# Cross-attention and a quantized feed-forward block: the order of loads, stores and row sums in a hand-written loop

## The chip, the cores and the metric

The kernel runs on one core of a Trainium2 chip. The time is device microseconds of one execution. A profiled execution gives a page and a trace beside it.

## The reference

The input x has 4 batches of 2048 rows of 512 values. Two layers follow one another.

```python
x = x + xattn(layernorm(x), ctx_1024, Wq, Wkv, Wout, bout)
x = x + ffn(layernorm(x), w1, b1, w2, b2, gamma, beta)
```

In the attention the mask lets a query i see only the keys j with `j % n_q == i`. There are 2048 queries and 154 keys, so query i < 154 sees one key, its own, and every other query sees none of them and averages all. The layer's result for a row of x is therefore a row that depends on the context alone: the row of value i for i < 154, the mean row for the rest. The kernel computes these rows once and adds them to x.

The feed-forward layer normalizes a row (with gamma and beta), quantizes it to whole numbers by its largest absolute value, multiplies by w1 (512 to 2048, weights quantized to -1, 0 and 1), rescales and adds b1, applies GELU, quantizes the 2048 values of the row in the same way, multiplies by w2 (2048 to 512), rescales, adds b2, and adds the result to x.

## The kernel before

The 8192 rows are 64 tiles of 128 rows, taken in the order `seq`. All constants stay in SBUF. Every engine runs its instructions in the order of a text: the strings BEGINNING, STEADY and ENDING hold words, and each word calls one function for one tile. BEGINNING prepares the weights and the context rows and runs up to tile 23. A loop over n = 24, 28, ... 52 runs STEADY, in which a number is counted from n: U2 is the word U for tile n+2. ENDING takes the last eight tiles. Nothing reorders the words afterwards. Words on different engines run side by side as their data allows; words on the same engine stand in line.

For one tile the words are, in the order of its life:

- L: load two tiles of x, 512 KB (`load_pair`, SyncE's DMA queue, L199). In STEADY, L14 loads tiles n+14 and n+15, and L16 loads n+16 and n+17.
- a: add the context row to x (`add_rows`, GpSimd, L269). S: mean and variance (VectorE, L276, L277). N: reciprocal roots for four tiles (GpSimd).
- k, e: normalize, gamma and beta (GpSimd, L323, L326, L327). R: largest value (VectorE, L355; for the last of four tiles also L361, L363). v: scales of four tiles (VectorE, L369, L371). X: add b2 to x (GpSimd, L349).
- Q: quantize the row (ScalarE, L375). T: transpose it by DMA to `xqT` (SyncE's queue, L386).
- I: put b1 into PSUM, in two halves (I n.half.vector; VectorE L545 or ScalarE L547). U: 16 matmuls with w1 (TensorE, L555).
- G: GELU, in two halves (ScalarE, L574). M: largest value of a half (VectorE, L586, then L600 to L603). D: a scale (GpSimd, L608).
- H: quantize 2048 values (ScalarE, L615). h: transpose them by DMA to `hqT`, 512 KB (SyncE's queue, L626).
- W: 16 matmuls with w2 (TensorE, L633). F: rescale and add to x (VectorE, L639). f: store the tile, 256 KB (SyncE's queue, L642).

Beside these, s and t load context rows for a later batch; they follow STEADY at n = 28 and 44 (s) and at n = 24 (t).

All DMAs of the loop are issued by SyncE, in the order of the words L, T, h, f, s and t, and each issue waits for its data. So a word that is not ready holds up those behind it. U of a tile needs its T; W needs its h.

Of the kernel before, what the change touches and what calls it, by code (L numbers as in the profile page):

```python
# [53 lines left out]
def xattn_ffn(ctx: ExitStack, tc, x, ctxT, WvT, Wout, bout, w1T, b1, w2T, b2, gamma, beta, out):  # L54
    nc = tc.nc
    B, S, D = x.shape
# [20 lines left out]
    for g, size in enumerate(sizes):  # L77
# [64 lines left out]
    """  # L142
    STEADY = """
        U0 W-2 G0.0 I1.0.1 G0.1 M0.0 Q2 k7 I1.1.0 T2 M0.1
        U1 L14 e7 L16 G1.0 X0 H0 M1.0 W-1 a13 I2.0.1 Q3 h0 D-1 S11 G1.1 a15 T3 R6 I2.1.0
        U2 N8 M1.1 G2.0 F-2 D0 R7 D1 a14 H1 W0 v4 I3.0.1 k9 G2.1 h1 X3 M2.0 I3.1.0 a12 F-1
        U3 Q4 M2.1 e9 I4.0.0 T4 S12 H2 F0 k8 W1 S13 X1 G3.0 h2 G3.1 M3.0 e8 I4.1.0 M3.1 Q5
        k10 T5 S14 H3 e10 f-2 f-1 F1 f0 R8 h3 R9 f1 X2 D2
    """
    ENDING = """  # L150
        U0 k7 W-2 I1.0.1 G0.0 e7 G0.1 M0.0 I1.1.0 M0.1 D-1 X1 Q2
# [622 lines left out]
```

## Time and profile before

| | |
|---|---|
| median of three runs | 523.04 us (521.98 to 523.38) |
| the profiled execution | 520.9 us, span 519.1 us |
| TensorE busy | 500.0 us |
| VectorE, ScalarE, GpSimd busy | 425.0, 420.4, 395.8 us |
| transposes of GELU rows (L626) | 65, median 4.4 us from issue to landing |
| loads of x (L199) | 32, median 5.4 us |
| stores (L642) | 64, median 2.5 us |
| granted TensorE clock | 0.997 |

Lines of a group give line, engine, operation, what it writes and reads, the count, then busy time and mean duration. In the chain of waits each piece has its start, its length and what it was; a timeline has start, length, engine, line and operation. A matmul of 512 columns follows the one before after 0.216 us in the trace although the page gives it 379 ns, since matmuls overlap; a busy TensorE is therefore not yet one without gaps.

### The profile page before, as it was taken

Reading aid. Unit: us, or ns where it says so; the run is one execution under the profiler, and the core shown is the slowest. Engines: PE = TensorE matmul, PEld = TensorE weight load, DVE = VectorE, ACT = ScalarE, POOL = GpSimd, SP = SyncE. Lnnn points to the kernel's source line nnn. Section 1 sums busy time; section 2 is a strip of 40 time slices with the busy share of each in tenths; the row PEclk is TensorE's granted clock in tenths of the full one; section 3 lists DMA queues with packets and bytes.
Section 4 is the critical chain, followed back from the end, with each engine's and each line's share of the span. In section 5 each row is a group of like instructions: output and inputs, shape, how many; then the busy total and the mean of one; then the engine's idle time right before and its main releaser. Section 6 shows DMA issues by size and latency. Waiting matters only on the chain.

```text
span 519.1 us, 6893 instructions
## 1 busy us (share of the span) xinstructions
PE 500.0 (96%) x2168; PEld 222.2 (43%) x2168; DVE 425.0 (82%) x757; ACT 420.4 (81%) x386; POOL 395.8 (76%) x512
## 2 busy tenths in 40 slices
PE   9796999999999999999989999999999999999996
PEld 4342444444444434444434444444444444444442
DVE  0478999999989797798988798989889978796762
ACT  1275999999898989878889697788787887998971
POOL 0048999999999979789969899996999599942120
PEclk9998999999999999999999999999999999999999
DMA  8998457797558899586696968679766876685654
GB/s 284 398 390 310 152 106 179 170 235 149 157 110 176 219 226 235 100 202 153 131 234 121 254 96 231 101 181 185 182 156 125 196 155 130 92 212 133 142 110 125
DMA packets 194114, 94.00 MB, mean 181 GB/s; under 512 B 170269, under 2 KB 170269, under 8 KB 194077
## 3 DMA queue, kind: packets, MB, share of 16 engines
q1 hardware_dynamic: 194076, 93.56, 74.7%
q8 instruction: 17, 0.28, 0.2%
q14 instruction: 21, 0.16, 0.1%
HBM read 34.55 MB, written 17.04 MB: 99 GB/s over the span
## 4 chain that ended last, share of the span: by engine, by line
PE 68%; DMA 18%; DVE 8%; ACT 2%; POOL 1%; issue 1%; SPq 0%; ACTq 0%; POOLq 0%; DVEq 0%
PE po L633 32%; PE ph L555 32%; DMA hqT<-hq 12%; DMA wo<-Wout_dram 3%; DVE m L586 2%; PE py L465 2%; DMA ws<-w2T_dram 2%; DVE ph L545 1%; ACT hid L574 1%; DVE m L355 1%; DMA wv<-WvT_dram 1%; POOL x L269 1%; DVE x L639 1%; DVE bn L276 1%; PE py_mean L465 1%
## 5 line engine op out<-in xcount | busy, mean ns | idle before, releaser
L633 PE MATMUL po<-w2q,hqT 128*128 128x512 f16 x1024 | 231.3, 379 | 5.2 <-DMA hqT<-hq 5.2
L555 PE MATMUL ph<-w1q,xqT 128*128 128x512 f16 x1024 | 231.5, 379 | 1.0 <-DMA xqT<-xqg 0.6
L586 DVE TENSOR_REDUCE m<-hid 128x1 f32<-128x1024 f32 (+1 forms) x130 | 153.4, 1194 | 39.7 <-ACT hid L574 39.2
L574 ACT ACTIVATE hid<-ph,d 128x1024 f32<-128x1024 f32 (+1 forms) x130 | 140.2, 1092 | 38.4 <-PE ph L555 26.8
L633 PEld LDWEIGHTS <-hqT 128*128 128x128 f16 x1024 | 99.1, 98 | 129.1 <-DMA hqT<-hq 11.3
L555 PEld LDWEIGHTS <-xqT 128*128 128x128 f16 x1024 | 100.1, 98 | 124.5 <-issue 2.8
L615 ACT ACTIVATE hq<-hid,i 128x2048 f16<-128x2048 f32 (+1 forms) x65 | 128.0, 1970 | 18.5 <-DVE i L603 8.8
L547 ACT ACTIVATE ph<-b_b,inv 128x1024 f32<-128x1024 f32 x91 | 100.5, 1112 | 1.2 <-POOL inv L369 0.8
L349 POOL TENSOR_TENSOR x<-x,b_b 128x512 f32<-128x512 f32 x59 | 74.8, 1270 | 0.0
L269 POOL TENSOR_TENSOR x<-x,mean 128x512 f32<-128x512 f32 x51 | 65.1, 1280 | 11.2 <-DMA x<-x_dram 9.5
L327 POOL TENSOR_TENSOR h<-h,beta_b 128x512 f32<-128x512 f32 x50 | 63.8, 1275 | 3.9
L326 POOL TENSOR_TENSOR h<-h,gamma_b 128x512 f32<-128x512 f32 x50 | 63.5, 1270 | 1.8
L639 DVE SCALAR_TENSOR_TENSOR x<-po,d,x 128x512 f32<-128x512 f32 x64 | 47.1, 739 | 10.9 <-PE po L633 10.6
L375 ACT ACTIVATE xqg<-h,s 128x512 f16<-128x512 f32 x64 | 45.2, 713 | 3.2 <-DVE s L363 3.2
L545 DVE TENSOR_SCALAR ph<-b_b,inv 128x1024 f32<-128x1024 f32 x37 | 47.3, 1277 | 0.0
L276 DVE BATCH_NORM_STATS2 bn<-x 128x6 f32<-128x512 f32 x64 | 43.6, 681 | 3.3 <-POOL x L269 3.2
L355 DVE TENSOR_REDUCE m<-h 128x1 f32<-128x512 f32 x64 | 41.9, 672 | 1.7 <-POOL h L327 1.4
L608 POOL TENSOR_TENSOR d<-mh,wm 128x1 f32<-128x1 f32 x64 | 12.6, 205 | 39.0 <-DVE mh L601 35.1
L323 POOL TENSOR_SCALAR h<-x,minus,rstd 128x512 f32<-128x512 f32 x50 | 38.4, 768 | 0.4
L436 PE MATMUL wps<-wo,wv 128*128 128x512 f32 x64 | 28.5, 597 | 1.8 <-DMA wv<-WvT_dram 1.4
L245 POOL TENSOR_SCALAR w1q<-wi 128x1024 f16<-128x1024 int16 x5 | 5.7, 1149 | 31.7 <-ACT wi L242 31.7
L251 DVE TENSOR_REDUCE part<-ws 128x1 f32<-128x1024 f32 x7 | 8.1, 1209 | 19.5 <-DMA ws<-w1T_dram 19.5
(75 smaller groups left out, 273.4 us busy)
## 6 DMA issues: line engine op xcount, KB each, us to landing
x<-x_dram SPq DMA_DIRECT2D x32, 512.0 KB, 5.4
out_dram<-x SPq DMA_DIRECT2D x64, 256.0 KB, 2.5
ws<-w1T_dram SPq DMA_DIRECT2D x8, 512.0 KB
ws<-w2T_dram SPq DMA_DIRECT2D x8, 512.0 KB, 8.7
wv<-WvT_dram SPq DMA_DIRECT2D x8, 256.0 KB, 7.8
wo<-Wout_dram SPq DMA_DIRECT2D x8, 256.0 KB, 6.6
ctx_sb<-ctxT_dram SPq DMA_DIRECT2D x1, 1232.0 KB
hqT<-hq SPq DMA_TRANSPOSE x65, 4.4
```

What stands on the lines that cost most here:

```text
L269: e.tensor_tensor(x_of(n), x_of(n), y, ALU.add)
L326: nc.gpsimd.tensor_tensor(normed[n], normed[n], gamma_b, ALU.mult)
L327: nc.gpsimd.tensor_tensor(normed[n], normed[n], beta_b, ALU.add)
L349: e.tensor_tensor(x_of(n), x_of(n), b2_b, ALU.add)
L545: nc.vector.tensor_scalar(ph, row, d, None, ALU.mult)
L547: nc.scalar.activation(ph, row, AF.Identity, bias=0.0, scale=d)
L555: nc.tensor.matmul(bank[i], xqT[n][:, k, :], w1q[:, k, i * 512 : (i + 1) * 512], start=False, stop=(k == KD - 1), skip_group_check=True,)
L574: nc.scalar.activation(hidden[n][:, i * w : (i + 1) * w], up_ps[n][half][:, lo : lo + w], AF.Gelu, bias=0.0, scale=deq1[g][:, j : j + 1],)
L586: nc.vector.tensor_reduce(m2[:, i : i + 1], hidden[n][:, i * w : (i + 1) * w], AX.X, ALU.max, apply_absolute_value=True,)
L615: nc.scalar.activation(hq[n][:, lo : lo + w], hidden[n][:, lo : lo + w], AF.Identity, bias=0.0, scale=inv2[n],)
L633: nc.tensor.matmul(po, hqT[n][:, k, :], w2q[:, k, :], start=(k == 0), stop=(k == KH - 1))
L639: nc.vector.scalar_tensor_tensor(t, down_ps.pop(n), deq2[n], t, ALU.mult, ALU.add)
```

## The change

Only the text STEADY changes. Before it, the loads L14 and L16 stand together near the start of U1, ahead of h0; after it, L14 stands behind h0 and L16 behind h1. The four sums of x with the row, `a13 a15 a14 a12` before, become `a12 a13 a14 a15`, in the same four places. The stores f-2 and f-1 move from behind T5 to behind h2, ahead of T5; f0 moves from ahead of h3 to behind it.

```diff
     STEADY = """
         U0 W-2 G0.0 I1.0.1 G0.1 M0.0 Q2 k7 I1.1.0 T2 M0.1
-        U1 L14 e7 L16 G1.0 X0 H0 M1.0 W-1 a13 I2.0.1 Q3 h0 D-1 S11 G1.1 a15 T3 R6 I2.1.0
-        U2 N8 M1.1 G2.0 F-2 D0 R7 D1 a14 H1 W0 v4 I3.0.1 k9 G2.1 h1 X3 M2.0 I3.1.0 a12 F-1
-        U3 Q4 M2.1 e9 I4.0.0 T4 S12 H2 F0 k8 W1 S13 X1 G3.0 h2 G3.1 M3.0 e8 I4.1.0 M3.1 Q5
-        k10 T5 S14 H3 e10 f-2 f-1 F1 f0 R8 h3 R9 f1 X2 D2
+        U1 e7 G1.0 X0 H0 M1.0 W-1 a12 I2.0.1 Q3 h0 L14 D-1 S11 G1.1 a13 T3 R6 I2.1.0
+        U2 N8 M1.1 G2.0 F-2 D0 R7 D1 a14 H1 W0 v4 I3.0.1 k9 G2.1 h1 L16 X3 M2.0 I3.1.0 a15
+        F-1
+        U3 Q4 M2.1 e9 I4.0.0 T4 S12 H2 F0 k8 W1 S13 X1 G3.0 h2 f-2 f-1 G3.1 M3.0 e8 I4.1.0
+        M3.1 Q5 k10 T5 S14 H3 e10 F1 R8 h3 f0 f1 R9 X2 D2
     """
```

SyncE's queue in one iteration, before and after:

```
before: T2 L14 L16 h0 T3 h1 T4 h2 T5 f-2 f-1 f0 h3 f1
after:  T2 h0 L14 T3 h1 L16 T4 h2 f-2 f-1 T5 h3 f0 f1
```

GpSimd's, before and after; VectorE, ScalarE and TensorE keep theirs:

```
before: k7 e7 X0 a13 D-1 a15 N8 D0 D1 a14 k9 X3 a12 e9 k8 X1 e8 k10 e10 X2 D2
after:  k7 e7 X0 a12 D-1 a13 N8 D0 D1 a14 k9 X3 a15 e9 k8 X1 e8 k10 e10 X2 D2
```

## The prediction

> **What bounds the kernel now.** I read the page first: its busy shares, its chain of waits and its DMA issues.
>
> ```profile
> PE 500.0 (96%) x2168; PEld 222.2 (43%) x2168; DVE 425.0 (82%) x757; ACT 420.4 (81%) x386; POOL 395.8 (76%) x512
> PE 68%; DMA 18%; DVE 8%; ACT 2%; POOL 1%; issue 1%; SPq 0%; ACTq 0%; POOLq 0%; DVEq 0%
> hqT<-hq SPq DMA_TRANSPOSE x65, 4.4
> ```
>
> TensorE sets the time; where it waits, the chain goes back through the transposes of GELU rows (hqT). So I listed the starts of all 2048 matmuls of L555 and L633 in the trace. They come in blocks of 16, each 3.455 us: one `U` (up) or one `W` (down). An iteration of the loop over STEADY has eight: U0 W-2 U1 W-1 U2 W0 U3 W1, at least 27.64 us. What the eight iterations (first tile n = 24, 28 ... 52) lose in gaps between matmuls is 0.71, 1.72, 0.66, 0.78, 0.49, 0.67, 0.58 and 0.36 us: 5.97 us in all. Past them the ENDING part loses only 0.44 us, at W63. No reordering inside the loop can gain more than 5.97 us.
>
> Then the chain of waits, one window with the 1.72 us and one typical iteration:
>
> ```profile
> 264.14 1.34 PE po L633 x7
> 265.48 7.08 DMA hqT<-hq
> 272.56 0.05 issue
> 272.60 3.63 PE po L633 x16
> ...
> 301.67 0.12 ACT hid L574
> 301.79 5.97 DMA hqT<-hq
> 307.76 0.05 issue
> 307.81 3.63 PE po L633 x16
> ```
>
> The first is h28 before W28 (the word h0 before W0). The second is h33 before W33 (h1 before W1). Both transposes took longer than the usual 4.4 us, for different reasons. For the first, SP's queue around it in the timeline:
>
> ```profile
> 261.95 0.40 SPq L520 DMA_DIRECT2D mean<-rest_dram  x1
> 262.45 1.19 SPq L386 DMA_TRANSPOSE xqT<-xqg  x1
> 263.69 1.08 SPq L199 DMA_DIRECT2D x<-x_dram  x2
> 265.48 4.17 SPq L626 DMA_TRANSPOSE hqT<-hq  x1
> ```
>
> h28 stands behind two loads of 512 KB. By the trace's semaphore records they land at 267.70 and 269.87, and h28 at 272.56, 2.69 after the second: one queue, served in order. This is the case that the change removes.
>
> For the second nothing stands ahead: SP had waited for ScalarE until 301.79. The packet records show what held it: a 16 KB instruction packet starts at 305.86 and takes 0.96 us; from 306.15 on, eleven packets of the transpose take 1.3 to 1.4 us instead of 0.02 and end together near 307.6, when a last string of packets, one at a time, is through. In the DMA view of the window 225 to 453 us:
>
> ```profile
> q8 instruction: 8, 0.13, 0.2%
> hqT<-hq SPq DMA_TRANSPOSE x32, 5.2
> ```
>
> Eight such packets in eight iterations, each 21.6 to 23.0 us after U0 starts, while h1 is under way (18.82 to 24.8). All eight h1 take 5.67 to 6.08 us.
>
> **The change part by part.** Engine times below are counted from the start of U0 of the iteration.
>
> *L14 and L16 behind h0 and h1.* h0 is issued when H0 ends on ScalarE, and H0 follows G1.0, which follows the first half of U1: 11.86 in all eight iterations. W0 is due at 17.27, so h0 may take 5.36 us. Where loads do not overlap it, it lands at 16.1 to 16.2 (4.3 us). It was late in three iterations: landings 18.94, 17.69, 17.70, costing 1.72, 0.47 and 0.48 us at W0. With the loads behind it these three go. What is late next is W1, two blocks on: h1 is issued at 18.82 in every iteration, because H1 follows G2.0 and that follows the first half of U2, whatever W0 did. It landed at 24.83, 24.70, 24.79, 24.90, 24.62, 24.80, 24.72 and 24.49; W1 starts 0.05 later and is due at 24.18 (seven blocks). So without W0's waits W1 alone would lose 0.70, 0.57, 0.66, 0.77, 0.49, 0.67, 0.59 and 0.36: 4.81 us. The gain is 5.97 - 4.81 = **1.16 us**, nearly all from n = 28; at n = 40 and 48 W1 takes over all that W0 gives back.
>
> *What now stands behind a load.* T3 (row transpose for U3) follows L14, T4 follows L16. The packet records of the load of pair 12 (BEGINNING, between h8 and T12) price a load in the queue: its packets run from 129.1 to 131.0, 1.9 us, about 0.5 of it before the first arrives. T3: h0 at 16.2, plus 1.9 and some 0.8 for T3, lands at 18.9; U3's weights are read at 20.5. Hidden, margin 1.6. T4 lands 0.4 to 0.6 after h1 now (1.37 at n = 48, which has no L16), so about 2.4 after; U4 follows W1, and its weights are read 3.3 after h1 has landed. Hidden, margin 0.9, the smallest of all. The transpose h2 starts at 24.4 to 26.8 and would land up to 1 us later, near 29.8; its user, the next W-2, is due at 31.7. Without the cover every 0.1 us costs 0.6, since six iterations have an L16.
>
> *Loads later, sums in tile order.* a13 and a15 become a12 and a13, whose rows came with the last iteration's L16: GpSimd no longer waits there. It did, in the waits of 225 to 453 us:
>
> ```profile
> POOL x L269 <- DMA x<-x_dram: 13.0, 4, 4.8
> ```
>
> Now a14 waits. Its place is free at about 16.4 (it started between 16.2 and 20.0), and L14 lands near 18.2. GpSimd then does what it did at n = 28 and 40, where a14 started at 18.3: its last word D2 ended near 34.8, and the next iteration's k7, at 6.6 after n = 40, delayed nobody. Some 26.5 us of work in 28.3: the wait comes out of slack. S12 no longer waits for a12 (up to 2.2 us on VectorE, off the path).
>
> *VectorE's small operations.* After R7 it scales four numbers (L361, L369, L371). At n = 44 one shows what happens when GpSimd adds rows at that moment:
>
> ```profile
> 384.59 1.27 POOL L269 TENSOR_TENSOR x<-x,mean 128x512 f32<-128x512 f32 x1
> 384.67 1.21 DVE L361 TENSOR_SCALAR m<-m 128x4 f32<-128x4 f32 x1
> 386.55 1.32 DVE L371 TENSOR_TENSOR d<-m,wm 128x4 f32<-128x4 f32 x1
> 386.58 1.27 POOL L349 TENSOR_TENSOR x<-x,b_b 128x512 f32<-128x512 f32 x1
> ```
>
> An operation of 0.2 us lasts until GpSimd's ends. That made I3.0.1 and so U3 late at n = 24 and 44 (0.14 and 0.58). With GpSimd idle from 16.4 to 18.2, R7 and v4 (16.1 to 17.5) are free of it. U3's lateness goes, but W1 still starts when h1 lands, so it is worth nothing; h2 and h3 move up to 2 us earlier on ScalarE.
>
> *Stores.* f-2 and f-1 stand ahead of T5, f0 behind h3 and F1. A store takes about 0.7 us of the queue; T5, which landed at 30.5 to 33.0, feeds a U5 due at 35.2. h3 loses one store ahead of it and lands 0.4 to 0.9 earlier; the next W-1 was covered by as little as 0.3. No cost.
>
> Sum: -1.16 us, from a profiled execution of 520.9 us (span 519.1). That execution is 2.1 us below the median of 523.04; I carry the difference over: 523.04 - 1.16 = **521.9 us**. If the eight h1 move by 0.15 us either way, the sum moves by 1.2.
>
> **The rivals.**
>
> *The median has more late h0 than the profile.* Those waits follow iterations in which VectorE or GpSimd ran late, so they may vary by execution; the 2.1 us are room for them, though they may as well lie outside the loop. All removed: 519.8.
>
> *W1's wait goes as well.* If it is T4, now issued 2.65 us after h1, and not the instruction packet, that holds h1 up, L16 takes its place and all 5.97 us go: 517.1. Against it: h24 has T27 issued right behind it and takes 4.33. The Trainium skill ("Runtime: NRT & Kernel Launch", section "Instruction fetch mechanics") has the refill of 16 KB blocks as mostly hidden; by that rule this rival would be the likelier one, and the 0.96 us packet inside each long h1 speaks against it.
>
> *U4 waits for T4 (slower).* L16 right behind h1, on an engine that is late already, may take more than 1.9 us. The load of pair 16, before the loop, landed 3.4 after the transpose ahead of it, at 186.78. At 3.4 T4 lands 3.9 after h1, 0.6 too late, in six iterations: +3.6 - 1.2 = +2.4, 525.4. It decides from a queue time of 2.8 us on; those of pairs 9, 10 and 12 landed 2.0 to 2.7 after it, and part of that is no queue time. The Trainium skill ("DMA: Bandwidth & Descriptors", section "Latency and other measured facts") gives HBM access 0.2 us on average and 2 us at high load; by the high figure a load would fall in this rival, by the average it would not, and the 0.5 us seen lies nearer the low one.
>
> *Nothing moves.* If h28 was late from the mean row ahead of it (landing at 265.72), not from the loads, the 1.16 stay: 523.0. Against it: the loads landed last.
>
> **How the numbers follow.** About 0.3% (1.57 us) is what a measurement can tell from no change, so faster is below 521.5. Forecast 0.50 (own range 520.7 to 523.0, about a third of it faster); hidden h0 waits 0.15; W1's wait gone 0.12; U4 late 0.18; nothing 0.05. Faster 0.17 + 0.15 + 0.12 = 0.44; slower 0.18; same 0.38. The range leaves out most of the W1 case and the worse half of the U4 case: 518.8 to 524.8.
>
> **What would show it.** Right: no gap before W0; h0 landing at 16.2; h1 at 24.5 to 24.9 and W1 right behind; a14 near 18.3; U4 without a gap. Wrong: h1 taking 4.4 us (faster), or U4 starting when T4 lands, or h1 held up by T3 behind L14 (slower).

## The result and the profile after

| | before | after |
|---|---|---|
| median, us | 522.61 (521.98 to 524.07, 6 runs) | 517.12 (516.13 to 518.15, 6 runs) |
| ratio of times | | 0.9888, interval 0.9871 to 0.9906 |
| profiled execution, us | 520.9 | 517.07 |
| span, us | 519.1 | 515.3 |
| lost between matmuls in the loop, us | 5.97 | 1.52 |
| granted TensorE clock | 0.997 | 0.993 |

The kernel is 5.5 us faster, outside the range of the prediction on the fast side. The page of after, its busy shares, its chain of waits and its row for the transposes of GELU rows:

```profile
PE 499.9 (97%) x2168; PEld 223.8 (43%) x2168; DVE 415.9 (81%) x757; ACT 419.7 (81%) x386; POOL 396.0 (77%) x512
PE 78%; DMA 11%; DVE 6%; issue 2%; POOL 1%; ACT 1%; SPq 1%; ACTq 0%; DVEq 0%; POOLq 0%
hqT<-hq SPq DMA_TRANSPOSE x65, 4.6
```

The work of TensorE is the same; the chain is on DMA for 11% instead of 18%. (The lines of the code have moved down by one: L634 is the down matmul, L556 the up matmul, L627 the transpose h, L200 the load.) By the starts of all matmuls, five of the eight iterations lose nothing at all: they last 27.63 us each. Three lose 0.67 (n = 40), 0.59 (48) and 0.26 (52), all three at W1, since h1 lands late there.

So both waits that the prediction showed for before are gone, W0's and W1's. The chain of waits of after where n = 28 had its 1.72 us (start, length, what):

```profile
264.11 3.45 PE po L634 x16
267.57 3.45 PE ph L556 x16
271.02 3.45 PE po L634 x16
274.47 3.45 PE ph L556 x16
277.93 3.45 PE po L634 x16
```

The third block is W28 and the last one W29; neither waits. SP's queue of the same stretch in the timeline (start, length, engine, line):

```profile
265.45 1.71 SPq L627 DMA_TRANSPOSE hqT<-hq  x1
267.22 1.21 SPq L200 DMA_DIRECT2D x<-x_dram  x1
268.53 1.19 SPq L387 DMA_TRANSPOSE xqT<-xqg  x1
272.41 1.83 SPq L627 DMA_TRANSPOSE hqT<-hq  x1
274.29 1.06 SPq L200 DMA_DIRECT2D x<-x_dram  x1
```

These are h28, L14, T31, h29, L16: the change does what it says. The transpose h29, issued at 18.82 after U28, lands at 23.43; in before it landed at 24.70. The instruction packets that the prediction made responsible are all still there. The DMA view of the loop, 226 to 449 us:

```profile
q8 instruction: 8, 0.13, 0.2%
hqT<-hq SPq DMA_TRANSPOSE x32, 4.7
```

Eight packets of 16 KB in eight iterations as before, at 22.7 to 22.9 after U0 in all but n = 52, and the median of the 32 transposes is 4.7 us instead of 5.2.

Outside the loop after's profiled execution lost more than before's: W15 and W16, whose text the change leaves alone, wait 2.08 us together instead of 1.36. That is why 4.45 us less lost in the loop make 3.8 us less of span.

### The profile page after: what moved, and what is told of

It is laid out like the page before. It is cut to its first block, busy times and chain, and to the rows that moved or that the text cites. A ratio compares the mean times of both kernels' runs of the same rounds, so it can differ in the third digit from the quotient of the medians.

```text
span 515.3 us, 6898 instructions
## 1 busy us (share of the span) xinstructions
PE 499.9 (97%) x2168; PEld 223.8 (43%) x2168; DVE 415.9 (81%) x757; ACT 419.7 (81%) x386; POOL 396.0 (77%) x512
## 4 chain that ended last, share of the span: by engine, by line
PE 78%; DMA 11%; DVE 6%; issue 2%; POOL 1%; ACT 1%; SPq 1%; ACTq 0%; DVEq 0%; POOLq 0%
PE ph L556 36%; PE po L634 36%; DMA hqT<-hq 7%; DMA ws<-w1T_dram 3%; PE wps L437 2%; PE py L466 2%; DVE m L587 1%; DVE part L252 1%; ACT hid L575 1%; POOL x L270 1%; DVE ph L546 1%; PE py_mean L466 1%; DMA xqT<-xqg 1%; DVE x L640 1%; DVE m L356 1%
## 5 line engine op out<-in xcount | busy, mean ns | idle before, releaser
L634 PE MATMUL po<-w2q,hqT 128*128 128x512 f16 x1024 | 231.2, 379 | 3.1 <-DMA hqT<-hq 3.0
L556 PE MATMUL ph<-w1q,xqT 128*128 128x512 f16 x1024 | 231.5, 379 | 0.5 <-DMA xqT<-xqg 0.5
L634 PEld LDWEIGHTS <-hqT 128*128 128x128 f16 x1024 | 99.6, 98 | 125.6 <-DMA hqT<-hq 6.5
L556 PEld LDWEIGHTS <-xqT 128*128 128x128 f16 x1024 | 100.1, 98 | 123.6 <-DMA xqT<-xqg 2.0
L324 POOL TENSOR_SCALAR h<-x,minus,rstd 128x512 f32<-128x512 f32 x50 | 38.4, 768 | 0.4
L437 PE MATMUL wps<-wo,wv 128*128 128x512 f32 x64 | 29.6, 620 | 0.8 <-DMA wv<-WvT_dram 0.8
L252 DVE TENSOR_REDUCE part<-ws 128x1 f32<-128x1024 f32 x7 | 8.1, 1209 | 18.9 <-DMA ws<-w1T_dram 18.9
```

The source lines that it names most:

```text
L556: nc.tensor.matmul(bank[i], xqT[n][:, k, :], w1q[:, k, i * 512 : (i + 1) * 512], start=False, stop=(k == KD - 1), skip_group_check=True,)
L634: nc.tensor.matmul(po, hqT[n][:, k, :], w2q[:, k, :], start=(k == 0), stop=(k == KH - 1))
```

## The experiments

The question was why h1 had come free although the packet had not. The theory made from the two traces, called A in the expectations: an instruction packet delays h1 only if another transpose stands right behind h1 in SP's queue. The rivals there lay the delay on one thing alone: B on the packet, as the prediction did, and C on the transpose T4 behind h1. That the loads no longer stand ahead of h0 is tested as well. All diffs are against the text named; only changed words are shown. The kernel before was run beside each group: 522.59 us (25 runs), 522.47 (13) and 522.47 (17).

**Only the neighbour of h1 put back.** Against the changed kernel, L16 goes from behind h1 to behind T4. Everything else stays as changed.

```diff
- h1 L16 X3
+ h1 X3
- T4 S12 H2
+ T4 L16 S12 H2
```

> The changed kernel with L16 moved from behind h1 to behind T4, so that T4 stands right behind h1 again. Theory A (collision): a 16 KB instruction packet stops one DMA engine just when T4, a transpose that all 16 engines work on together, has begun, and h1's completion is held up behind T4. Then h1 lands 24.6 to 24.9 us after U0 again, W1 loses 0.4 to 0.8 us in nearly every iteration, and the time goes from 517.1 to about 521. Theory B (the prediction's: the packet alone delays h1, whatever stands behind it): nothing changes, 517. Theory C (T4 right behind h1 is enough, packet or not) expects the same as A here.

Measured: 520.80 us (520.07 to 521.37, 10 runs), ratio 0.9961 (0.9941 to 0.9982). The loop loses 5.09 us, all of it at W1: 0.52, 0.66, 0.65, 0.79, 0.55, 0.67, 0.71, 0.55. Its chain of waits at n = 32, where after has nothing:

```profile
301.54 0.12 ACT hid L575
301.67 5.96 DMA hqT<-hq
307.62 0.05 issue
307.67 3.63 PE po L634 x16
```

Before had 5.97 us in this place. One word, L16, ahead of T4 or behind it, decides W1's wait. It is not the absence of the loads ahead of h0: W0 waits nowhere in this kernel either.

**T4 later, the rest as before.** Against the kernel before, Q4 comes after I4.0.0 on ScalarE, so that T4 is issued 3.69 us after h1 (22.51) instead of 2.65 (21.47). The packet is left alone.

```diff
- U3 Q4 M2.1 e9 I4.0.0 T4
+ U3 M2.1 e9 I4.0.0 Q4 T4
```

> The kernel before with one word moved: Q4 behind I4.0.0 on ScalarE, so that T4 is issued about 1.1 us later (22.6 instead of 21.5 us after U0). Loads and stores stay as before. A and C: h1 lands at 23.2 to 23.9, W1 loses nothing, only the waits for h0 stay (about 2.7 us in the profile): 519 to 520. B: h1 still lands at 24.5 to 24.9, 522 to 523.

Measured: 520.86 us (517.56 to 524.01, 10 runs), ratio 0.9974 (0.9946 to 1.0002): no time that can be told from the kernel before. The mechanism shows even so. h1 lands at 23.16 to 23.92 in seven iterations (24.46 in the eighth, n = 52), and W1 waits for it only there, 0.33 us. The forecast of 519 to 520 was missed nevertheless: the profiled execution (522.97 us) gave the gain back, most of it at W0, where the loads still stand ahead of h0. Its loop loses 6.7 us, 4.28 of it at n = 28:

```profile
266.13 7.94 DMA hqT<-hq
274.07 0.05 issue
274.12 5.31 PE po L633 x16
```

TensorE waited 2.59 us for h28, and the 16 matmuls behind that took 5.31 us instead of 3.63.

**The packet moved away, T4 left where it was.** Against the kernel before, 64 matmuls of one column, of no use to the result, run in the preparation. With their weight loads they are 128 more instructions for TensorE, and the 16 KB packets of the loop then start 7.5 to 8.7 us after U0, outside h1.

```diff
+    nil = constant([P, P], F16, "nil")
+    nc.gpsimd.memset(nil, 0.0)
+    def spend(t):
+        for _ in range(32):
+            nc.tensor.matmul(t, nil, nil[:, 0:1], start=True, stop=True)
+    spend(idle[:, 0:1])
...
+            if i == 1:
+                spend(py["tot", i][:, 1:2])
```

> The kernel before with 64 one-column matmuls on zeros (128 TensorE instructions with their weight loads), half at the start and half where TensorE waits before the py_rest rows; their results are not used. The loop's text is as before, but the 16 KB instruction packet is fetched half an iteration earlier in it, near 9 us after U0 instead of 22.9. A and B: h1 lands at 23.1 to 23.6 and W1 loses nothing; left are h0's waits: 519 to 520 if the start costs nothing (up to 2 us if it does). C: h1 lands at 24.6 to 24.9 as before, 522.6 or more.

Measured: h1 lands at 23.16 to 23.85 in all eight iterations, with T4 right behind it as in before, and W1 never waits. So T4 alone does no harm. The time, though: 523.35 us (519.31 to 524.88, 10 runs), ratio 0.9994 (0.9962 to 1.0026), where 519 to 520 was expected. The profiled execution was the shortest of the ten, 519.31 us; it loses 2.80 us in the loop, 2.16 at W0 of n = 28 and 0.64 at W-1 of n = 40.

The same kernel was profiled again, to see one of its longer executions:

> The kernel with the packet shifted, for a second trace: its timed runs lay between 519.3 and 524.9, its first trace was of the fastest. A: h1 again at 23.1 to 23.9 and W1 never late; what makes a slower run is W0 waiting for h0 behind two loads, above all at n = 28, by 2.2 us and more, and then slow matmuls for some 2 us, as in the second trace of the kernel before. If W1 is late again, the packet's place does not decide.

Measured: 524.69 us. h1 lands at 23.18 to 24.34 and W1 never waits for it; but W28 waits 3.30 us for h28, and the matmuls after that lose 2.92 more at half the clock. In the windows view (us, busy PE, PEld, DVE, ACT, POOL, then the granted clock, DMA share, GB/s):

```profile
275.60:282.10 6.50, 6.49 (x17) 2.40 (x18) 2.56 (x7) 3.82 (x4) 6.42 (x7) 0.54 0.75 143
```

17 matmuls in 6.5 us at a clock of 0.54. What W1 gave, W0 took, and W-1 another 1.43 us (n = 28 and 40).

**The step as the semaphores and packets show it.** The records of DMA packets and of semaphores for the transpose h33 (n = 32), in us after U0. A transpose ends with 32 packets of 4 bytes, and its semaphore is raised 16 times; it has landed with the last.

```
                 next in   issued  T4's first  16 KB packet   last 4-byte   the 16 increments
                 the queue         packet      starts, takes  packet of h1
before           T4        21.47   22.65       22.89  0.96    22.88         23.49, then 24.67 to 24.79
t4_first         T4        21.47   22.65       22.87  0.93    22.86         23.53, then 24.64 to 24.78
q4_later         T4        22.51   23.68       22.64  0.93    22.64         22.97 to 23.10, then 23.34
shift            T4        21.47   22.65       none near      22.63         22.97 to 23.20
after            L16       20.80   24.37       22.83  0.96    22.82         23.13 to 23.27, then 23.43
store_between    f-2       20.87   23.12       22.88  0.94    22.77         23.08 to 23.24, then 23.40
```

In every row h1's packets (2048 of 256 bytes, then the small ones) are all out by 22.9, ahead of the instruction packet or level with it; the 512 packets of 256 bytes behind them are T4's. What differs is when the increments come. In before, T4's packets begin near 22.65 and are under way while the instruction packet runs, from 22.89 to 23.85. Eleven of them, begun at 23.2 to 23.35, take 1.3 to 1.4 us instead of 0.02. They end at 24.62, when a string of T4's last 33 packets, one after another from 23.84 on, is almost through, and only then do fifteen of h1's sixteen increments come. In shift T4 begins as early, but no instruction packet comes, and all increments are there by 23.20.

Where T4's first packet comes at 23.12 or later, behind a load, behind a store or 1.04 us late by itself (q4_later), only one increment is late, by 0.2 us. So it is T4's start that decides, and not the kind of transfer ahead of it. In store_between the slow packets are still there (six of T4's take 1.2 to 1.45 us); they hold up T4 itself until about 25.3, and U4 is due at 27.63 only. The Trainium skill ("DMA: Bandwidth & Descriptors", section "Why a DMA increments its semaphore by 16 and not by 1") says that each engine's increment lands only after that engine's data. That agrees with h1's last data being held, too, though no record here shows where the increments wait.

**One part of the change: L16 alone.** Against the kernel before, only L16 goes behind h1. L14, the stores and the sums stay.

```diff
- U1 L14 e7 L16 G1.0
+ U1 L14 e7 G1.0
- h1 X3
+ h1 L16 X3
```

> The kernel before with L16 alone moved behind h1; L14, the sums and the stores stay. A and C: h1 lands at 23.4 to 23.6 in the six iterations that have an L16, W1 loses only at n = 48 and 52 (0.6 and 0.4), h0 with one load ahead is late by at most 0.4 in n = 28: about 518. B: W1 as before, W0's waits smaller: 521.5.

Measured: 518.70 us (518.36 to 521.40, 6 runs), ratio 0.9917 (0.9887 to 0.9947). W1 is late by h1 only in the two iterations without an L16 (n = 48 and 52: 0.58 and 0.71). W0 of n = 28 waits 0.76 us, more than the 0.4 expected. The trace is of one of the two longer executions of the six (521.09 us): its loop loses 3.4 us, but the loop begins 2.8 us later than in the first trace of before. By the medians this one move brings 3.9 of the 5.5 us (2.8 to 5.9 by the interval).

**The other part: both loads ahead of h0 again, stores and sums as changed.**

```diff
- U1 e7 G1.0
+ U1 L14 e7 L16 G1.0
- h0 L14 D-1
+ h0 D-1
- h1 L16 X3
+ h1 X3
```

> The changed kernel with both loads back where they were before it (ahead of h0); the sums in tile order and the stores stay as changed. What is left against the kernel before is sums and stores alone. If these two count for nothing, as forecast: 522 to 523, with the scatter of the kernel before (519 to 526), W1 losing 0.4 to 0.8 wherever W0 did not wait. If they count: the time lies off 522.6 by what they are worth, at most 2 us either way.

Measured: 520.68 us (519.76 to 523.20, 10 runs), ratio 0.9968 (0.9944 to 0.9992). W1 waits in seven iterations (0.31 to 0.68 us); in the eighth, n = 32, W0 waits 1.20. The loop loses 5.20 us. Stores and sums together are worth about 1.8 us (0.4 to 2.9 by the interval); the loads make the rest. The sums by themselves, put into the order of the tiles in the kernel before:

```diff
- W-1 a13 ... G1.1 a15 ... I3.1.0 a12
+ W-1 a12 ... G1.1 a13 ... I3.1.0 a15
```

> The kernel before with only the sums in tile order (a12 a13 a14 a15); loads ahead of h0 and stores as before. The version with sums and stores changed gained 1.8 us over the kernel before. If it is the sums (GpSimd no longer waits for L14 in U1, so it runs evenly and a late iteration does not follow): 520.5 to 521.2, a14 at the same time in all iterations. If it is the stores: 522.5.

Measured: 522.14 us (519.34 to 525.25, 12 runs), ratio 0.9991 (0.9966 to 1.0016); its trace loses 6.15 us in the loop. Nothing that can be told from before. Whether the 1.8 us are the stores' alone or need both stays open: the stores were not tried alone, and the two intervals overlap.

**Something else between h1 and T4.** Against the changed kernel, the store f-2 stands behind h1 in all iterations, and L16 behind T4.

```diff
- h1 L16 X3
+ h1 f-2 X3
- T4 S12 H2
+ T4 L16 S12 H2
- h2 f-2 f-1
+ h2 f-1
```

> The changed kernel with f-2 in the place of L16 behind h1, and L16 behind T4: a store of 256 KB stands between h1 and T4, in all eight iterations (L16 exists in six). Theory A (T4 under way while the instruction packet holds one engine is what delays h1): a store is a spacer as a load is; h1 lands at 23.2 to 23.8 in all iterations, also in n = 48 and 52 where the changed kernel lost 0.59 and 0.26, and T4 lands near 25.5: 516 to 517, some 0.5 to 1 us under the changed kernel. If the spacer is too short (the packet runs to 23.85, T4 would start near 23.3), h1 lands at 24.6 again and the time is near 521.

Measured: 515.75 us (514.96 to 516.15, 4 runs), ratio 0.9855 (0.9825 to 0.9885). h1 lands at 23.33 to 23.52 in seven iterations, n = 40 and 48 among them, where after loses 0.67 and 0.59. The chain around W41 (the last line):

```profile
353.23 3.45 PE po L634 x16
356.69 3.45 PE ph L556 x16
360.14 3.45 PE po L634 x16
```

The loop loses 0.27 us, at n = 52 alone. There the packet comes at 21.64, in the middle of h1, and h1 lands at 24.39 although f-2 stands behind it; the expectation had h1 free there too. For the packet on the end of h1 the transfer behind h1 need not be a load: a store does the same. This kernel and after were then run on one chip:

> The version with f-2 between h1 and T4 and L16 behind T4, again, beside the changed kernel. By A it saves W1's losses at n = 40 and 48, about 1.2 us: 515.3 to 516.3, below the changed kernel in every pair of medians. If the first result was the chip's and not the kernel's, both lie within 0.5 us.

> The changed kernel again, beside the next one on the same chip: 516.5 to 517.7.

Measured: 516.82 us (515.22 to 518.27), ratio 0.9888 (0.9853 to 0.9923), beside 517.45 us (517.12 to 518.84), ratio 0.9907 (0.9877 to 0.9937), 6 runs each. The medians stand in the order expected, but 0.6 us apart with overlapping runs, and not at the 515.3 to 516.3 that was expected of the first. The traces are clear (0.23 us lost in the loop beside 1.26); that the time is better is not shown.

**The packets moved in the changed kernel.** The 64 small matmuls again, in after:

> The changed kernel with the same 128 TensorE instructions ahead of the loop, so that the instruction packet comes near 9 us after U0. A: h1 lands at 23.1 to 23.4 in all iterations and W1's last losses (0.67, 0.59 and 0.26 at n = 40, 48, 52) go: 515.5 to 516.5, if the extra instructions cost nothing at the start; up to 2 us more if they do. The packet may now meet T2, which has room: U2 comes 3 us later. C (T4 alone): 517 or more, W1 late in n = 48 and 52 as before.

Measured: 516.30 us (516.11 to 516.63, 4 runs), ratio 0.9870 (0.9836 to 0.9904). The DMA view of the loop gives the transposes their old 4.4 us:

```profile
hqT<-hq SPq DMA_TRANSPOSE x32, 4.4
```

The loop loses nothing. h1 lands by 23.77 in all iterations, and at 23.21 and 23.25 at n = 48 and 52, where T4 stands right behind it. So what after still loses comes with the packets. At n = 48 no L16 stands between, and T4 meets the packet (22.84) as in before. At n = 52 the packet came at 21.2, in the middle of h1. At n = 40 another instruction packet (8 KB, 0.55 us, at 19.89) fell within h1 ahead of the 16 KB one (22.72); fifteen increments were there by 23.21 but the last only at 24.80. In after_shift a packet of 8 KB came at 20.30 in that iteration without the other, and h1 landed at 23.06.

**Before once more.** To see where its median stands above the first profile:

> The kernel before once more, for a second trace of it. Its 25 timed runs lie between 519.3 and 525.7, and the first trace was of a run of 520.9. If loads ahead of h0 make the scatter, this trace shows the same 0.4 to 0.8 at W1 and other waits of W0, and its loop's lost time differs from the first trace's 5.97 by about as much as its time does. If the scatter lies outside the loop, the loop loses 5 to 6.5 again.

Measured: 523.72 us, 2.8 above the first profiled execution; the loop loses 8.41 us instead of 5.97. Seven iterations lose 0.48 to 0.78 each, much like the first trace's. n = 28 loses 3.88 instead of 1.72: W28 waits 2.19 us for h28, which lands at 19.41, and its matmuls then run at half the clock for 3.41 us and lose 1.68. In the windows view, W28 and the 6.8 us behind it:

```profile
273.30:278.60 5.30, 5.20 (x17) 2.07 (x18) 3.76 (x7) 5.09 (x5) 5.30 (x7) 0.68 0.65 124
278.60:285.40 6.80, 6.80 (x33) 3.08 (x32) 4.75 (x11) 3.93 (x5) 6.64 (x7) 1.00 0.42 80
```

The clock (third figure from the right) is 0.68 on the mean over W28's 5.3 us, and 1.00 again behind it. Not all scatter is the loop's: the two traces of before reach U24 at 225.3 and 225.6 us, but the two of after at 226.0 and 228.0.

## Why the prediction was wrong

**The step that failed** is the first of the parts: "without W0's waits W1 alone would lose ... 4.81 us". The 4.81 were taken to stay; after lost 1.52 at W1, and 1.26 in the second trace of it. The prediction saw the packet inside every long h1, and took it for a cause that is enough by itself. It misread one row: the "eleven packets of the transpose" that it gave to h1 start from 306.15 on, 23.18 us after U0, and the last packet of h1 had started at 22.88. They are T4's. It also used h24, with T27 right behind and 4.33 us long, to dismiss T4. But h24 shows only that a transpose behind is not enough; that the packet alone is not enough, no row of before could show, because all eight h1 with a packet also had T4 behind them. The two stood together in all rows, and the change parted them. The runs show that both are needed when the packet falls on the end of h1: packet and T4 together (t4_first, 5.09 us lost at W1), packet without T4's packets right behind (nothing lost in five iterations of after and seven of store_between), T4 without the packet (shift, nothing at W1). A packet in the middle of h1 is enough alone, as the prediction had it: that is the 0.27 us of store_between at n = 52.

**The rival "W1's wait goes as well"**, 517.1 us, named the right wait, neighbour and time. Its condition, T4 "and not the instruction packet", was half wrong. That its 517.1 met the measured 517.12 is luck: of the 5.97 us that it let go, 4.45 went, 0.6 was lost again outside the loop, and the 2.1 us named next made up the rest. The rule beside it, that refills of instructions are mostly hidden (the Trainium skill, "Runtime: NRT & Kernel Launch", section "Instruction fetch mechanics"), holds here for after's five clean iterations, and not for t4_first, where each refill costs 0.52 to 0.79 us.

**The second term that was off** is the 2.1 us between the profiled execution and the median, carried over as a constant. After's profiled execution is at its median (517.07 and 517.12). The rival "the median has more late h0 than the profile" said as much: before_2 shows 2.16 us more lost at n = 28, and a part that it did not foresee, matmuls at half the clock behind a long wait. Nor is after's match a rule: its second trace, of 518.84 us, lies 1.4 us above the median of its group. The two terms make up the miss of 4.8 us: 4.81 - 1.52 = 3.3 at W1; 2.1 not carried over; less the 0.6 that after's trace lost elsewhere, nearly all at W15 and W16.

How the 5.5 us divide, by medians: 522.6 before, 520.8 with all but L16's place (t4_first), 517.1 with it: 1.8 and 3.7. The traces give 5.09 - 1.52 = 3.6 for the second step. For the first, t4_first lost 0.9 less in the loop than the first trace of before and 3.3 less than the second.

**W0 and h0**: right. h0 lands at 16.12 to 16.19 and W0 never waits.

**T3 and T4**: right in what follows from them. T3 lands at 18.6 to 18.7 behind an L14 (forecast 18.9). T4 was forecast 2.4 after h1 and lands up to 3.2 after it (at 26.5 to 26.7), since L16 takes longer in the queue than the 1.9 us taken for it: it lands near 26.1, some 5.3 after its issue. The rival "U4 waits for T4" was not near all the same: U4 is due at 27.63, 0.9 after the latest T4, and at n = 40, where h1 is late, T4 lands at 26.63 as elsewhere.

**GpSimd and a14**: right. a14 starts at 18.13 to 18.35 (forecast 18.2), and the wait moved to it:

```profile
POOL x L270 <- DMA x<-x_dram: 8.3, 7, 1.8
```

Seven waits of up to 1.8 us instead of four of up to 4.8. The last word D2 starts at 34.4 to 34.6 in these iterations and delays nobody.

**VectorE's small operations**: right. At n = 44 the two that took 1.21 and 1.32 us in before, with GpSimd waiting beside them:

```profile
381.64 0.17 DVE L362 TENSOR_SCALAR m<-m 128x4 f32<-128x4 f32 x1
382.13 0.15 DVE L372 TENSOR_TENSOR d<-m,wm 128x4 f32<-128x4 f32 x1
383.02 1.27 POOL L270 TENSOR_TENSOR x<-x,mean 128x512 f32<-128x512 f32 x1 [1.71 <-DMA x<-x_dram]
```

U3 starts on time, 20.72, in all eight iterations. The prediction called that worth nothing since W1 would wait; with W1's wait gone it is worth its 0.14 and 0.58 us at n = 24 and 44, which W1's numbers already hold.

**h2, h3 and the stores**: h2 lands at 28.7 to 29.3, not up to 1 us later but as early as the earliest of before; h3 at 34.8 to 35.4 instead of 35.7 to 38.4. No store costs TensorE anything.

## What to carry to other kernels

If two suspects stand together in every row of a trace, none of those rows says that one of them is enough; look for the row that parts them, and if there is none, give the case in which the change parts them a larger chance. In a queue of transposes that the next matmuls wait for, what begins right behind a transpose can decide when it completes: a load or a store between two transposes cost nothing here, and the load freed about 3.7 us. In the kernel with both loads still ahead of h0, delaying T4 or shifting the packet freed h1 as well, but W0 gave the gain back. And when the profiled execution differs from the median, profile the kernel again before the difference is carried over as a constant.

## What the hardware showed that was not expected

A transpose whose packets are all out is not yet complete. With another transpose right behind it and an instruction packet of 0.93 to 0.96 us on one engine, fifteen of its sixteen increments came 1.5 us later (24.67 to 24.79 instead of 23.13 to 23.27 for h33). A load or a store in between, or T4 issued 1.04 us later, took that away: T4's first packet then came at 23.12 to 24.37 instead of 22.65. Without the packet two neighbouring transposes pay nothing (shift, increments by 23.20).

A wait of TensorE can cost more than its length. Behind waits of 2.19 us (before_2), 2.59 (q4_later) and 3.30 (shift_2) the granted clock was halved for 3.41, 3.41 and 6.83 us, and the matmuls lost 1.68, 1.67 and 2.92 us. Behind waits of 1.72 (before), 1.78 (sums_only) and 2.16 us (shift) it was not. The Trainium skill ("TensorE: Matmul & The Clock Gate", section "What's actually happening") gives a free-running window of 3.413 us for the clock gate, and the halved stretches are one and two such windows long. The Trainium skill's statement there that an idle window of about 3.4 us brings the low clock does not fit as a bound here: 2.19 us of waiting was enough. In before_2 the stretches at full clock between two changes last 13.65, 27.31 and 221.87 us, which are 4, 8 and 65 times 3.413, so the changes fall on a fixed grid: in before_2 and q4_later the halving begins at the next step of it, 0.59 and 0.50 us after the wait has ended. The longest waits without a halved clock are the 2.16 us of shift, which fall on two steps, and 2.10 us at W15 of shift_2, within one. Whether the whole wait counts or its share of one step, these runs do not decide.
